# A four-layer graph network on one core: a fixed order for the hyperbolic preparation and end, and for the attention layer with its two GRUs

## The chip, the core and the metric

The kernel runs on one core of a Trainium2 chip. The metric is device time in microseconds (us) of one execution. Below, PE is the matrix engine (TensorE), DVE the vector engine (VectorE), ACT the scalar engine (ScalarE), POOL GpSimd, and SP the engine that issues most transfers.

## What is computed

N = 3327 nodes with D = 64 features and a 0/1 adjacency matrix of about 16 neighbours per row. Four layers follow each other, each of the form x = x + layer(relu(layernorm(x)), adj):

```python
# layers 0 and 3: hyperbolic, c = 1 and c = 1 / r**2
x_t = logmap0(h, c)
adj_att = sigmoid(x_t @ w[:D] + (x_t @ w[D:]).T + b) * adj
support = einsum('ij,ijd->id', adj_att, logmap(h[:, None], h[None], c))
out = proj(expmap(h, support, c), c)
# layer 1: decay
rank = cumsum(adj != 0, axis=1)              # weight 0.5 ** (deg - rank)
out = w @ (h @ weight) + bias
# layer 2: two GRU cells on sums over neighbours
edge_output = gru(concat(A_pos @ h, A_neg @ h), h, ...)   # adj has no negatives here
node_output = gru(softmax_mean(h @ W_gat), h, ...)
out = d_edge[:, None] * edge_output + d_node[:, None] * node_output
```

With a 0/1 matrix the attention is the mean of h @ W_gat over the neighbours without the diagonal, and the second half of the first GRU's input is zero.

## The kernel before

Nodes are padded to 3328 = 26 tiles of 128 (T = 26). X keeps the features as [128, 26, 64] in SBUF; the two halves of the tiles (HALVES, 13 each) are often handled one after the other. Shapes on DVE are thus 128x832 (half), 128x1664 (all), and 128x26 for one number per node.

`hyperbolic_series` (layers 0 and 3) has three parts. The preparation normalises (`norm_relu`, lines 111 to 129), computes |h|^2 (L386 to L388), scales to Xr (L399), splits it into two fp16 parts (L400, L405), transposes these to columns on PE (`to_columns16`, L407), computes the attention scalars left and right, spreads left over partitions into leftB (L452 to L463), and transposes a second set of columns, XE. Here the framework's scheduler orders the engines' instructions by its own costs. The series then runs over 4 column chunks times 26 row tiles with an order written out by hand (`manual_schedule`): sigmoid on ACT (L517), times adjacency on POOL (L519), two pairs of products on PE (L530, L531), a square on ACT (L537), two passes on DVE (L542, L543), and sums on PE (L552, L560). In layer 0 the adjacency tile comes by DMA (L505, 4 buffers), in layer 3 from fp8 masks that are already in SBUF. The end (L643 to L742) works on 128x26 numbers and then updates X by four wide passes per part (L739, L740); its square roots (`sqrt_`, L94) are corrected by one Newton step on DVE and are then inverted where 1/sqrt is wanted.

`plain_decay` (layer 1) loads 52 half-row tiles of the matrix (832 KB each, 4 buffers, L1259), makes fp8 masks on DVE (L1287), counts on DVE that entries are 0 or 1 (`zeros`, L1207; for 13 tiles, LATE, this is put off into layer 2, which loads them again, L1394), and runs cumulative counts, an exponential on ACT (L1300) and sums on PE (L1311). Its order is written out by hand. Before it, `norm_relu` and `split2` (L164) make the fp16 parts of h; POOL adds the bias to X in one instruction (L1362).

`plain_gat` (layer 2) normalises again, checks degrees (L1415, L1416), inverts them by DVE reciprocals (L1426), sums the masks times h on PE (L1407, 26 blocks of 16 products), and then runs two GRUs, each over 4 column blocks of 416 (L1437 to L1475): products (L1453, L1463), sigmoids (L1455), tanh (L1467), state (L1465 to L1475); for the second GRU first a product with W_gat (L1447) and a copy on ACT (L1448). All this is ordered by the scheduler. The GRU weights come by POOL's DMA queue at the start of layer 1 (`gru_weights`, L1209). `ball` (L274) prepares the constants of a hyperbolic layer, for layer 3 on DVE (L295 to L301). A last comparison of counts decides whether a slow fallback runs; it doesn't with these inputs.

## Time and profile before

| what | us |
|---|---|
| median of 3 runs (827.92 to 830.69) | 829.16 |
| the profiled execution's own time | 831.17 |
| its span (first to last instruction) | 829.5 |
| layer 0, preparation up to the first square's input | 0 to 33.5 |
| layer 0, series | 33.5 to 265.9 |
| layer 0, end | 265.9 to 284.3 |
| layer 1, first masks, normalising | 284.3 to 299.7 |
| layer 1, sweep up to its last product | 299.7 to 428.8 |
| layer 2, up to the first product of the mask sums | 428.8 to 457.8 |
| layer 2, mask sums | 457.8 to 497.0 |
| layer 2, GRUs; then the update of X | 497.0 to 538.7; to 543.0 |
| layer 3, preparation | 543.0 to 571.2 |
| layer 3, series | 571.2 to 801.9 |
| layer 3, end, and the close of the program | 801.9 to 822.1; to 829.5 |

A table row's borders are the starts of instructions in the timeline. Over the span PE is busy 662.2 us, DVE 721.5, ACT 562.0, POOL 419.0; these are averages over stages with different limits. In a timeline line the columns are start, busy time, engine, line of the kernel, operation, output and input with shapes, the count of merged instructions, and in brackets the idle time before and what ended it. The lines of a stretch table give the stretch, its length, then the busy time and number of instructions of PE, PE's weight loads, DVE, ACT and POOL, the granted PE clock, the DMA share and GB/s.

### The profile page before, as it was taken

The page shows a single profiled execution, that of the slowest core. Times are in us where ns is not written, and L with a number is a line of the kernel's source. Part 1 is how long each engine was busy: PE and PEld are TensorE (multiplying, and loading weights), DVE is VectorE, ACT ScalarE, POOL GpSimd, SP SyncE. Part 2 cuts the span into 40 slices and gives each one's busy share as a digit, 9 for nine tenths or more (in the row PEclk, how much of TensorE's full clock was granted, in tenths as well). Part 3 has the DMA queues.
Part 4 walks back from the last instruction along what each step waited for, and adds up shares of the span by engine and source line. Part 5 has one row for each costly group of instructions (what it writes and reads, how often), then busy time and mean ns, then how long its engine had stood idle before and what let it go on. Part 6 is the DMA issues. An engine that isn't in the chain of part 4 may idle for free.

```text
span 829.5 us, 11810 instructions
## 1 busy us (share of the span) xinstructions
PE 662.2 (80%) x4228; PEld 251.2 (30%) x4228; DVE 721.5 (87%) x1013; ACT 562.0 (68%) x684; POOL 419.0 (51%) x283
## 2 busy tenths in 40 slices
PE   0889999999896059989970997618999999998940
PEld 0422233333331024435430662204222333333310
DVE  7689999999997999999989946796999999999966
ACT  3878888888884167777761306448888888888850
POOL 2499989989985310002300000004787777787720
PEclk9999999999999569999995899958999999999985
DMA  2577766767662639999943630002001001000001
GB/s 42 167 235 227 204 204 191 238 182 204 190 191 66 225 126 339 349 347 333 338 170 126 220 113 1 0 0 48 1 2 35 1 1 35 0 2 1 0 4 44
DMA packets 56887, 107.86 MB, mean 130 GB/s; under 512 B 8305, under 2 KB 32817, under 8 KB 56817
## 3 DMA queue, kind: packets, MB, share of 16 engines
q1 hardware_dynamic: 51712, 106.68, 40.2%
q10 hardware_dynamic: 4656, 0.08, 0.3%
q8 instruction: 35, 0.57, 0.3%
q0 software_dynamic: 448, 0.24, 0.1%
q14 instruction: 36, 0.29, 0.1%
HBM read 103.73 MB, written 0.88 MB: 126 GB/s over the span
## 4 chain that ended last, share of the span: by engine, by line
DVE 65%; PE 14%; DMA 7%; ACT 6%; issue 5%; POOL 2%; ACTq 1%; DVEq 0%; POOLq 0%
DVE sig L543 22%; DVE slot L542 20%; DMA adj<-in 7%; DVE same L1207 5%; PE acc L1407 5%; DVE mask L1287 3%; POOL sig L519 2%; PE slot L552 2%; ACT y L537 1%; DVE deg L1426 1%; PE cnt L1294 1%; DVE X L740 1%; DVE prod L739 1%; PE slot L560 1%; DVE ln_v L123 1%
## 5 line engine op out<-in xcount | busy, mean ns | idle before, releaser
L537 ACT ACTIVATE y<-slot,shift_c 128x768 f32<-128x768 f32 (+1 forms) x208 | 197.6, 950 | 69.7 <-ACT sig L517 48.1
L543 DVE TENSOR_TENSOR sig<-slot,sig 128x768 f32<-128x768 f32 (+1 forms) x208 | 213.2, 1025 | 24.7 <-POOL sig L519 2.7
L542 DVE SCALAR_TENSOR_TENSOR slot<-y,slot 128x768 f32<-128x768 f32 (+1 forms) x208 | 212.1, 1020 | 9.0 <-ACT y L537 8.9
L519 POOL TENSOR_TENSOR sig<-adj,sig 128x768 f32<-128x768 f32 (+1 forms) x104 | 201.8, 1962 | 24.8 <-ACT sig L517 14.7
L517 ACT ACTIVATE sig<-leftB,right 128x768 f32<-128x768 f32 (+1 forms) x208 | 204.1, 981 | 0.2
L519 POOL TENSOR_TENSOR sig<-mask,sig 128x768 f32<-128x768 fp8e4 (+1 forms) x104 | 174.6, 1680 | 57.2 <-ACT sig L517 53.1
L552 PE MATMUL slot<-sig,Xr 128*64 128x384 f32 (+1 forms) x832 | 187.2, 538 | 18.3 <-DVE sig L543 18.3
L530 PE MATMUL slot<-XC,XT 128*128 128x384 f16 (+1 forms) x416 | 142.1, 342 | 5.0 <-DVE sig L543 3.3
L531 PE MATMUL slot<-XF,XE 73*128 73x384 f16 (+1 forms) x416 | 141.4, 340 | 0.0
L1300 ACT ACTIVATE w<-cnt,ebias 128x832 bf16<-128x832 f32 x104 | 93.8, 950 | 32.4 <-PE cnt L1294 32.4
L1207 DVE TENSOR_SCALAR_CACHE_REDUCE same<-adj 128x1664 bf16<-128x1664 f32 x52 | 97.7, 1880 | 3.5 <-DMA adj<-in 3.5
L560 PE MATMUL slot<-sig,X 128*32 128x384 f32 (+1 forms) x832 | 95.0, 529 | 0.0
L468 POOL COPY Xp<-Xe 128x234 f16<-128x234 f16 x2 | 0.8, 415 | 160.1 <-DVE XT L414 146.4
L552 PEld LDWEIGHTS slot<-sig,Xr 128*64 128x64 f32 x832 | 42.9, 135 | 123.9 <-DVE sig L543 85.2
L1294 PE MATMUL cnt<-mask,after 128*128 128x416 fp8e4 x208 | 54.8, 347 | 25.3 <-DVE mask L1287 22.6
L178 POOL TENSOR_TENSOR mask<-mask,offdiag 128x128 fp8e4<-128x128 fp8e4 x26 | 16.8, 666 | 105.4 <-PE cnt L1294 104.2
L530 PEld LDWEIGHTS <-XT 128*128 128x128 f16 x416 | 40.6, 98 | 94.7 <-issue 68.8
L1294 PE MATMUL cnt<-mask,rest 128*128 128x416 fp8e4 x208 | 55.0, 347 | 12.5 <-ACT w L1300 12.5
L1287 DVE TENSOR_SCALAR mask<-adj 128x1664 fp8e4<-128x1664 f32 x52 | 53.3, 1031 | 6.7 <-DMA adj<-in 6.6
L531 PEld LDWEIGHTS <-XE 73*128 73x128 f16 x416 | 40.7, 98 | 33.3 <-issue 9.3
L1311 PE MATMUL acc<-w,h 128*64 128x416 bf16 x416 | 47.2, 349 | 0.0
L1407 PE MATMUL acc<-mask,h 128*64 128x416 fp8e4 x416 | 38.3, 346 | 0.1
(293 smaller groups left out, 547.7 us busy)
## 6 DMA issues: line engine op xcount, KB each, us to landing
adj<-in SPq DMA_DIRECT2D x65, 832.0 KB, 6.9
adj<-in SPq DMA_DIRECT2D x78, 384.0 KB, 3.9
adj<-in SPq DMA_DIRECT2D x27, 512.0 KB, 4.7
leftB<-left SPq DMA_DIRECT2D x6, 384.0 KB, 3.9
XC<-XT SPq DMA_DIRECT2D x12, 96.0 KB, 3.0
X<-in SPq DMA_DIRECT2D x1, 832.0 KB, 4.5
out<-X SPq DMA_DIRECT2D x2, 416.0 KB, 2.4
XF<-XT SPq DMA_DIRECT2D x6, 96.0 KB, 2.7
```

What stands on the lines that cost most here:

```text
L517: A.activation(sig, leftB[c], AF.Sigmoid, bias=right[:, b:b + 1])
L519: G.tensor_tensor(sig, adj, sig, op=OP.mult)
L530: PE.matmul(L[:, o, :c[1] * P], XT[:, rows], XC[c][:, o, :], start=True, stop=False)
L531: PE.matmul(L[:, o, :c[1] * P], XE[:KE, rows], XF[c][:, o, :], start=False, stop=True)
L537: A.activation(ys[k], Ls[k][:, :, :c[1] * P], AF.Square, scale=-0.5 / SX ** 2, bias=shift_c)
L542: V.scalar_tensor_tensor(L, y, G3, L, op0=OP.add, op1=OP.mult)
L543: V.tensor_mul(sig, L, sig)
L552: PE.matmul(acc[c][o * D:(o + 1) * D, 0, :n], Xr[:, b, :], sigs[k][:, o, :], start=b == 0, stop=b == T - 1)
L560: PE.matmul(acc[c][q:q + 32, 1, :n], X0[:, b - 1 + i, :], w[:, o, :], start=b == 1, stop=b == T - 1, tile_position=(0, q))
L1207: V.tensor_scalar(same, adj, 0.0, 0.0, op0=OP.is_equal, op1=OP.add, accum_out=count)
L1294: PE.matmul(cnt[o][:, h, :BK], w, cols(k, o, h), start=w is after and steps[k][1] == T - 1, stop=True, skip_group_check=True)
L1300: A.activation(ws[k][:, o, :, :], cnt[o][:, :, :BK], AF.Exp, scale=-LN2, bias=ebias)
```

## The change

1. Hyperbolic preparation (both layers) goes into `manual_schedule` for ACT, DVE, PE and POOL. It no longer writes relu(H)/sd: R = max(H, 0) and its squares are summed, and 1/sd goes into the factor of Xr. `inverse_root` gives 1/sqrt directly with one Newton step. The fp16 copy into Xe goes from ACT to DVE. leftB is made from left itself instead of from its transposed copy, half of it copied by DVE. The small work for E, F and z is put between the DVE copies of the transposed columns. Numbers that the end needs are computed here. The first four adjacency tiles of layer 0 are loaded ahead of it; X comes in two transfers.
2. The end: fewer 128x26 steps, `inverse_root`, the Sqrt table loaded before in layer 3, X updated in halves, one product of the second half on ACT.
3. Weights of layers 1 and 2 come by SP's queue at the program's start, ahead of the first adjacency tiles; the constants of layer 3 are made on POOL in step 3 of the sweep.
4. Decay: 7 buffers instead of 4; bias added in 13 pieces on POOL in steps 3 to 15; second half normalised first, the lower fp16 part of the first half made in step 1; the degree total comes from ACT's accumulator.
5. Attention: fixed order for ACT, DVE and PE; 3 buffers for the late tiles; normalising first; W_gat is multiplied into the second GRU's weights ahead of the mask sums (the product L1447 goes); the degree check and 1/degree go to ACT (Relu with accumulator, Ln, Exp) with one Newton step on DVE; the half of the nodes that the mask sums need first is normalised first.
6. GRUs: the eight steps become a pipeline: products, sigmoids and the input of tanh of step u, with tanh and state of step u - 1.

```diff
+    def inverse_root(pool, src, name, root=None):
+        s0 = pool.tile(list(src.shape), F32, name=name) if root is None else root
+        if root is None:
+            A.activation(s0, src, AF.Sqrt)
+        q = pool.tile(list(src.shape), F32, name=name + "_q")
+        V.reciprocal(s0, s0)
+        V.scalar_tensor_tensor(q, src, -0.5, s0, op0=OP.mult, op1=OP.mult)
+        V.tensor_mul(q, q, s0)
+        V.scalar_tensor_tensor(s0, q, 1.5, s0, op0=OP.add, op1=OP.mult)
+        return s0
...
@@ hyperbolic_series, preparation
+            if masks is None:
+                for k in range(4):
+                    load(k)
-                norm_relu(tp, H)
...
+                    V.tensor_scalar(R[:, ts, :], H[:, ts, :], 0.0, None, op0=OP.max)
+                    A.activation(sr[:, ts, :], R[:, ts, :], AF.Square)
...
+                sd = inverse_root(tp, v, "sd", sd)
...
+                V.scalar_tensor_tensor(ia2, ia, 2.0, sd, op0=OP.mult, op1=OP.mult)
...
-                    V.tensor_mul(Xr[:, ts, :], H[:, ts, :], wide(ia2[:, ts]))
+                    V.tensor_mul(Xr[:, ts, :], R[:, ts, :], wide(ia2[:, ts]))
...
-                to_columns16(XT, Xp[:, :, :2 * D], P, 1)
+                to_columns16(XT, Xp[:, :, :2 * D], P, 1,
+                             (of_x0, of_e, of_f, lambda: V.tensor_copy(Xe[:, :, :D], hi), of_z))
...
+                to_columns16(XE, Xe, KE + 9, 0, (lambda: None, of_left))
...
@@ hyperbolic_series, end
+                last = HALVES[1]
+                extra = tp.tile([P, T // 2, D], F32, name="extra")
+                for k in range(T // 2):
+                    t = last.start + k
+                    A.activation(extra[:, k, :], M[:, t, :], AF.Copy, scale=am[:, t:t + 1])
...
@@ plain_decay
-                adjs[k] = wk.tile([P, 2, CW], F32, name="adj", bufs=4)
+                adjs[k] = wk.tile([P, 2, CW], F32, name="adj", bufs=AHEAD)      # AHEAD = 7
...
-                    if k == 4:
-                        G.tensor_tensor(X, X, bias[:, None, :].to_broadcast([P, T, D]), op=OP.add)
+                    if k == 1:
+                        late()
+                    if 3 <= k < 3 + T // 2:
+                        ts = slice(2 * (k - 3), 2 * (k - 2))
+                        G.tensor_tensor(X[:, ts, :], X[:, ts, :], bias[:, None, :].to_broadcast([P, 2, D]), op=OP.add)
...
@@ plain_gat
+                norm_relu(tp, hn, H.rearrange("p k o d -> p o k d"), order=(1, 0),
+                          then=lambda o: split2(*[p[:, :, o, :] for p in parts], H[:, :, o, :]))
+                PE.transpose(pt[:D, :D], wg, ident[:D, :D])
+                A.activation(wgT, pt[:D, :D], AF.Copy)
+                PE.matmul(pt[:D, :3 * D], wgT, wx[:D, :, :].rearrange("k g m -> k (g m)"), start=True, stop=True)
...
+                def inverse():
...
+                    V.tensor_scalar(deg, deg, 1.0, None, op0=OP.max)
+                    A.activation(few, deg, AF.Relu, bias=hundred, accum_out=ok[:, 3:])
+                    A.activation(r0, deg, AF.Ln)
+                    A.activation(r0, r0, AF.Exp, scale=-1.0)
+                    table_of(AF.Sigmoid, r0[:, :1])
+                    V.scalar_tensor_tensor(deg, deg, -1.0, r0, op0=OP.mult, op1=OP.mult)
+                    V.scalar_tensor_tensor(deg, deg, 2.0, r0, op0=OP.add, op1=OP.mult)
+                todo = {T - 4: lambda: turn(0), T - 6: lambda: degrees(0), T - 8: lambda: turn(4),
+                        T - 9: lambda: degrees(1), T - 11: lambda: turn(8), T - 12: lambda: degrees(2),
+                        T - 14: lambda: turn(12), T - 15: lambda: degrees(3), T - 17: inverse}
...
+                take(0)
+                for u in range(K + 2):
+                    if u < K:
+                        products(u)
+                    if u == 0:
+                        take(1)
+                    if u < K:
+                        sigmoids(u)
+                    if u == 0:
+                        take(2)
+                        take(3)
+                    if 0 <= u - 1 < K:
+                        tanh(u - 1)
+                    if u < K:
+                        before_tanh(u)
+                    if u < C:
+                        take2(u)
+                    if 0 <= u - 1 < K:
+                        state(u - 1)
...
-        nc.sync.dma_start(X, x.rearrange("p (t d) -> p t d", d=D))
+        for ts in HALVES:
+            nc.sync.dma_start(X[:, ts, :], x.rearrange("p (t d) -> p t d", d=D)[:, ts, :])
```

The new functions of the attention layer: `turn(t0)` is four transposes of H on PE and five copies on ACT; `degrees(k)` two products on PE and one subtraction on DVE; `take(k)` two ACT copies of the mask sums and one DVE product with 1/degree; `take2(k)` two ACT copies of that product; `products(u)` 8 products on PE into four of the eight PSUM banks in turn; `state(u)` three (first GRU) or four DVE passes.

## The prediction

> **What bounds the kernel now.** I read the chain of work that ended last, then busy time by stage, then the timeline of each stage that the change touches. The page's chain:
>
> ```profile
> DVE 65%; PE 14%; DMA 7%; ACT 6%; issue 5%; POOL 2%; ACTq 1%; DVEq 0%; POOLq 0%
> DVE sig L543 22%; DVE slot L542 20%; DMA adj<-in 7%; DVE same L1207 5%; PE acc L1407 5%; DVE mask L1287 3%; POOL sig L519 2%; PE slot L552 2%; ACT y L537 1%; DVE deg L1426 1%; PE cnt L1294 1%; DVE X L740 1%; DVE prod L739 1%; PE slot L560 1%; DVE ln_v L123 1%
> ```
>
> Over 40% is the two series, which the change leaves alone. The gains must lie between them; busy time by stage:
>
> ```profile
> 34.70:265.90 231.20, 215.63 (x1265) 67.93 (x1262) 211.01 (x224) 189.70 (x222) 207.03 (x112) 1.00 0.68 198
> 265.90:284.30 18.40, 0.00 (x0) 0.00 (x0) 16.95 (x72) 1.73 (x3) 10.15 (x17) 0.53 0.58 202
> 299.70:428.90 129.20, 125.58 (x840) 56.92 (x839) 119.71 (x131) 96.50 (x109) 16.81 (x26) 0.98 0.87 304
> 428.90:457.70 28.80, 5.15 (x29) 3.51 (x29) 27.78 (x35) 6.47 (x11) 0.00 (x0) 0.65 0.41 148
> 497.00:543.00 46.00, 31.19 (x163) 10.29 (x160) 31.54 (x57) 24.19 (x42) 0.00 (x0) 0.93 0.00 0
> ```
>
> From 428.9 to 457.7 PE does 5 us of work while DVE is full: the mask sums wait for DVE. From 497 no engine is full: the GRUs wait step by step. Timeline of DVE before the mask sums, its wait in the GRUs, the hidden stall in layer 1, and the table switches of the last end:
>
> ```profile
> 429.30 1.89 DVE L1415 TENSOR_SCALAR_CACHE_REDUCE few<-deg 128x1664 bf16<-128x1664 f32 x1 [2.56 <-ACT deg L1316]
> 431.12 1.88 DVE L1416 TENSOR_REDUCE zo<-deg 128x1 f32<-128x1664 f32 x1
> 443.49 2.74 DVE L1426 RECIPROCAL deg<-deg 128x416 f32<-128x416 f32 x1
> 524.32 0.65 DVE L1465 SCALAR_TENSOR_TENSOR nn<-ph,gb,spr 128x416 f32<-128x416 f32 x1 [0.68 <-PE ph L1463]
> 526.36 0.59 DVE L1469 TENSOR_TENSOR o<-hP,nn 128x416 f32<-128x416 f32 x1 [0.77 <-ACT nn L1467]
> 290.45 3.69 POOL L1362 TENSOR_TENSOR X<-X,bias 128x1664 f32<-128x1664 f32 x1 [8.01 <-DVE H L120]
> 292.38 1.79 DVE L124 TENSOR_SCALAR ln_v<-ln_v 128x26 f32<-128x26 f32 x1
> 804.76 1.28 ACT L98 ACT_TABLE_LOAD   x1 [2.89 <-DVE t L684]
> 806.29 1.28 ACT L687 ACT_TABLE_LOAD   x1
> ```
>
> A 128x26 step takes 0.18 us, yet L124 took 1.79: it ended as the bias addition did.
>
> **The Trainium skill.** "GPSIMD Engine Reference", section 1, says POOL shares its SBUF interfaces with DVE, contended by DVE's 2-port modes: L124 agrees, 1.61 us lost. "VectorE: DVE Perf Modes", section "The perf-mode tier table", gives fp32 tensor_scalar twice the rate of tensor_tensor: L1287 1.03 us against L1207's 1.88 for 1664 elements agrees, so R = max(H, 0) costs 0.5 us per half where L128 cost 0.98. "ScalarE: Activation LUTs", section "What ACT_TABLE_LOAD costs", gives 1283 ns plus a drain; the trace has 1.28 us and no drain (the next activation at 806.29 + 1.30), so I use 1.28. Its section "Table sets: the hidden batching unit" has ln and exp in one set; no run here shows it yet, so one load, two at the other end.
>
> **The change part by part**, against the profiled 831.17 us (span 829.5, 1.7 around it). On DVE a step that needs the one before starts 0.22 us after it, an independent one 0.10, a half (128x832) takes 0.98 (starts in the timeline).
>
> *Layer 0, preparation.* Now 5.36 (X landed) to 33.46 (first square). X in halves: 0.9 earlier (one 832 KB transfer lands in 4.5 us, a 416 KB one in 2.4, the second queued). Up to the second fp16 part: two passes L128 (1.95) become R (1.0), 0.95 saved; of the root and two reciprocals 0.8 goes beside sums: together 1.8. Then it is given back: in fixed order DVE does the dependent chain of E, F, z (of_x0 7 x 0.22, of_e and of_f 0.45 each, Xe 0.55, of_z 1.4, about 4.4 us) between copies of XT, where the scheduler now spaces 19 such steps at 0.1; and six of the seven XE groups, ahead of it now, come behind the leftB products on PE, 1.4. Before, ACT's Xe copy (1.58) and table load held its XT copies, which goes. Balance after the 1.8: +2.1. So +0.3 without, and -0.6 with X's 0.9. Then the first tiles: DVE idles 0.56 + 1.06 + 0.96 before three L543 between 43 and 51 us, POOL having waited for adjacency that was issued at 29.3; loaded ahead, about 1.5 goes, the rest is POOL's diag work. The 16 weight transfers ahead of these loads cost SP some 0.6 us each, 10 us; loads from 12 us on are hidden up to 33. **-2.1.**
>
> *Layer 0, end.* 265.93 to tanh 3.9 becomes 2.6 (kb, bx, bk precomputed; 9 dependent steps instead of 15); rr removes reciprocal and one product after tanh, 0.55; the last root 2.5 becomes 1.7 (inverse_root: one reciprocal, not two); the wide passes 7.4 become 7 x 0.98 = 6.9, ACT making the eighth (13 short activations at 0.25 = 3.3, hidden by 5.9 of DVE; uncovered it would cost the 1.0 that it saves). 1.3 + 0.55 + 0.8 + 0.5, rounded: **-3.3.**
>
> *Layer 1.* The bias leaves the path: -1.6; the lower part of the first half moves into step 1 of the sweep (-1.0, +1.0 there). In the sweep DVE does 48 more masks than the two made earlier, 50 x 0.94, and 39 checks x 1.80, 117.3, and additions 1.0; it waited 6.6 for adjacency (8 times) and 0.6 for PE. With 7 buffers and 33 us before the sweep, 9 tiles are in instead of 6; at 345 GB/s a tile takes 2.47 us against DVE's 2.37: the queue shrinks 0.1 x 43 = 4.3 us, less than it holds. So the 6.6 goes; next late is PE, 52 x 2.335 = 121.4 from about 296.5, and the pace of masks. 13 bias pieces (3.69 / 13 = 0.28 each) can hold a mask each: 0 to 3.7, I take 1. 1.6 + 6.6 - 1.0 rounds to **-7.3**.
>
> *Up to the mask sums.* With the sweep's last product at 428.8 as zero of time, X is final at 432.8 instead of about 434.1, L1415 and L1416 (3.77) gone from before it; the late tile's check (1.9, and 0.6 of waiting) goes behind; normalising undisturbed takes 8.0 to L128's start (542.96 to 550.98 in layer 3), so 440.8 instead of 453.85, the four reciprocals (10.9), L1424 and L1425 being out of it. PE's start doesn't gain all of it: its product with wgT waits for an ACT copy that stands behind the copy of the second half (H1 1.0, hi 0.95, lo 1.0, H0 1.0, hi 0.95: 445.9), then 0.7: 446.6 instead of 457.76. **-11.2.**
>
> *Mask sums.* 39.2, less 1.2 of waiting, plus 8 degree products 0.7: **-0.5**, end 485.3.
>
> *GRUs.* DVE's own steps: 4 takes 2.1, input of tanh 8 x 1.2, states 4 x 1.8 + 4 x 2.4: 28.5 us, where 41.7 passed. But DVE comes late: degrees(3) is on PE behind block 15 (472.3); then a check 1.8, maximum 1.0, and DVE waits for ACT's Relu, load, Ln, Exp (1.6 + 1.3 + 1.6 + 1.5 = 6.0; two loads 7.3), then 2 x 1.8, then the five last checks 9.3: 495.4, some 10 us after PE ended. Behind it stand the takes; step 1's products wait for take(3), as they use the banks of the sums. Takes to 497.5, tanh inputs of steps 0 and 1 and first state to 502.9, then 6 x 1.2 + 3 x 1.8 + 4 x 2.4 = 22.2, and 1.4 of bubbles and tail: 526.5, 41.2 after PE's end. **-0.5**; without the lateness it would be -6.
>
> *Layer 3.* Preparation as layer 0 without the halves, constants now ready: saves 1.8, gives 2.3 back: **+0.5** (bounds -2.5 if DVE's chain hides, +3). End: one table load and step savings up to tanh 1.9, last root 0.85, wide passes 0.95: **-3.7.** POOL's constants and memset cover: DVE work that doesn't need them.
>
> Sum -2.1 - 3.3 - 7.3 - 11.2 - 0.5 - 0.5 + 0.5 - 3.7 = -28.1. The profiled execution would take 803.1; the median stands 2.0 lower: 801.
>
> **The rivals.**
> *Fixed order costs* (809): each preparation gives back 3 more, and PE, not DMA, ends the sweep (2.3 x 52 plus a slow first step), so only 5 of 7.3 come: -28.1 + 6 + 2 = -20. For: only waits of 0.1 to 0.7 us are left to the scheduler there. Against: PE busy 125.6 includes slow-clock products before 304.
> *DVE in time* (793): Ln and Exp overlap the checks, so the GRUs gain 6, and the preparations 1.5 each: -37. Against: DVE's queue is in order.
> *Not what it says* (817): the pipeline and early mask sums are held by bank reuse; half of the 11.2 and 5 of the sweep lost: -12 to -18, -14 taken.
> *Slower* (835): PE's clock. In each series PE is busy 215.6 of 231.2 us at a granted 1.00; with fewer pauses before, the clock could fall. At 0.866 PE would need 249 per series, 17.8 more than now, twice 35.6, against 28.1 gained: about +7. It decides from 215.6/x = 245, a clock of 0.88. The page shows 0.9 or above all through both series but in slices at their borders: improbable.
>
> **The numbers.** Forecast 801: 0.47; fixed order 0.24; DVE in time 0.18; not what it says 0.07; slower 0.04. The range takes in the second and third with the unknown costs, 791 to 812. A measurement can tell some 0.3% (2.5 us) from no change. Faster 0.95, same 0.01, slower 0.04.
>
> **What would show it.** Right: L1426 and L1447 gone; first mask-sum product 17 to 19 us after the sweep's last (28.98 now); no DMA wait of L1287 over 0.5 us; DVE's last late check ending after the last mask-sum product, then GRU passes back to back; no L98 table load between 801.9 and tanh; the eight wide passes seven on DVE. Wrong: a preparation over 31 us from X to the first square; DVE waiting inside the GRU states; PE's clock under 0.9 in a series; a slow end that the chain gives to ACT.

## The result and the profile after

| kernel | median us | range, runs | ratio to before, 95% interval |
|---|---|---|---|
| before, same chip | 828.54 | 827.54 to 830.69, 4 | |
| changed | 819.63 | 818.34 to 820.25, 4 | 0.9882 [0.9868, 0.9897] |

Faster by 8.9 us in the medians. The forecast was 801: right in sign, but less than a third of the gain came. The profiled execution took 818.34 us (span 816.6), 12.8 less than the profiled one of before, which lay 2.6 above its median (831.17). First the chain of the changed kernel, then its stretches, with the columns as before.

```profile
DVE 31%; PE 7%; ACT 4%; issue 3%; DMA 1%; DVEq 0%; SPq 0%; ACTq 0%
```

```profile
36.21:268.38 232.17, 218.35 (x1268) 68.59 (x1265) 211.07 (x224) 190.82 (x224) 208.32 (x112) 0.99 0.66 190
268.38:283.85 15.47, 0.00 (x0) 0.00 (x0) 14.01 (x61) 4.94 (x16) 0.00 (x0) 0.53 0.91 346
296.79:425.33 128.54, 124.74 (x840) 56.89 (x839) 121.52 (x133) 97.48 (x113) 19.54 (x33) 0.99 0.79 286
425.33:443.63 18.30, 2.90 (x17) 2.03 (x18) 12.54 (x21) 7.09 (x12) 0.00 (x0) 0.71 0.37 140
484.58:531.13 46.55, 25.41 (x147) 8.84 (x144) 40.48 (x69) 22.99 (x41) 0.79 (x1) 0.79 0.11 37
```

The chain can be followed back over less than half of the span this time, so the stages carry the reading. The stretch ahead of the mask sums shrank from 28.80 to 18.30 as forecast. The sweep didn't: 128.54 against 129.20. In the last stretch DVE is now busy 40.48 of 46.55, where it had 31.54 of 46.00. Then the timeline, in the places shown of before:

```profile
291.89 0.18 DVE L138 TENSOR_SCALAR ln_v<-ln_v 128x26 f32<-128x26 f32 x1
293.72 1.25 DVE L143 SCALAR_TENSOR_TENSOR H<-H,ln_sd 128x832 f32<-128x832 f32 x1
295.65 5.69 POOL L1415 TENSOR_TENSOR X<-X,bias 128x128 f32<-128x128 f32 x8
480.80 1.89 DVE L1507 SCALAR_TENSOR_TENSOR deg<-deg,ln_sq 128x1664 f32<-128x1664 f32 x1 [7.70 <-ACT ln_sq L1505]
495.61 1.89 DVE L1248 TENSOR_SCALAR_CACHE_REDUCE same<-adj 128x1664 bf16<-128x1664 f32 x1 [2.35 <-DMA adj<-in]
497.43 1.58 DVE L1539 SCALAR_TENSOR_TENSOR deg<-bank,deg 128x416 f32<-128x416 f32 x3
796.97 1.28 ACT L119 ACT_TABLE_LOAD   x1
798.50 0.19 DVE L742 TENSOR_TENSOR th<-th,ti 128x26 f32<-128x26 f32 x1 [1.46 <-ACT spare L119]
```

The 1.79 of `ln_v` is 0.18: that stall is gone. The two passes L1415, L1416 and the reciprocals L1426 of before are gone, but DVE now waits 7.70 for ACT's inverse and 1.10 and 2.35 for two transfers, and reaches the takes at 497.43, 13 us after the mask sums. In the last end a wait of 1.46 is new. The ledger, from the timelines of the two profiled executions:

| stage | before | after | change | forecast |
|---|---|---|---|---|
| layer 0, to the first square | 33.46 | 36.21 | +2.75 | -0.6 |
| layer 0, series | 232.47 | 232.17 | -0.3 | -1.5 |
| layer 0, end | 18.41 | 15.47 | -2.9 | -3.3 |
| layer 1, first mask to last product | 144.44 | 141.48 | -3.0 | -7.3 |
| up to the first mask sum | 28.98 | 18.30 | -10.7 | -11.2 |
| mask sums | 39.24 | 40.95 | +1.7 | -0.5 |
| GRUs to the update of X | 41.84 | 42.42 | +0.6 | -0.5 |
| layer 3, preparation | 28.28 | 30.30 | +2.0 | +0.5 |
| layer 3, series | 230.94 | 231.72 | +0.8 | 0 |
| layer 3, end | 19.96 | 17.65 | -2.3 | -3.7 |
| update of X; close of the program | 4.12; 7.36 | 4.13; 5.80 | -1.6 | 0 |

That is -12.9 of span against -28.1. The mask sums end here where ACT takes the first of them, 0.5 before PE's last product ends, and layer 3's end begins at 802.18 in the kernel before. The close of the program is 1.6 shorter: this was not forecast, and why is not known. It took 7.4 and 7.6 us in the two profiles of the kernel before and of its variant below, and 5.5 to 6.0 in all others.

### The profile page after: what moved, and what is told of

Its sections match the earlier page's. It is cut to its first block, busy times and chain, and to the rows that moved or that the text cites. A ratio compares the mean times of both kernels' runs of the same rounds, so it can differ in the third digit from the quotient of the medians.

```text
span 816.6 us, 11802 instructions
## 1 busy us (share of the span) xinstructions
PE 659.8 (81%) x4215; PEld 252.1 (31%) x4215; DVE 709.1 (87%) x985; ACT 576.2 (71%) x729; POOL 416.1 (51%) x296
## 5 line engine op out<-in xcount | busy, mean ns | idle before, releaser
L577 POOL TENSOR_TENSOR sig<-adj,sig 128x768 f32<-128x768 f32 (+1 forms) x104 | 201.9, 1962 | 28.1 <-ACT sig L575 26.0
L191 POOL TENSOR_TENSOR mask<-mask,offdiag 128x128 fp8e4<-128x128 fp8e4 x26 | 15.0, 594 | 97.9 <-PE cnt L1333 97.9
L1518 PE MATMUL bank<-mask,h 128*64 128x416 fp8e4 x416 | 39.7, 348 | 0.0
```

The lines of the kernel that those rows point to most:

```text
L577: G.tensor_tensor(sig, adj, sig, op=OP.mult)
```

## The experiments

Every kernel is the changed one with the edit shown, unless said otherwise. Stage lengths are from each kernel's own profile; times are medians, with the ratio to the kernel before on the same chip.

### Yardstick: the changed kernel again

> The changed kernel once more, unedited, beside the others on one chip: what its stages do from run to run. From the runs so far: the first square between 36.2 and 37.6 us (the copies and transposes of the preparation ran at a varying granted clock), layer 1 between 141 and 144.5, the whole 818 to 822.

Measured: 819.45 us, 0.9889 [0.9873, 0.9906]. First square at 37.45, layer 1 143.1, the stretch up to the mask sums 19.7 (18.3 in the first profile), GRUs and ends as in the first profile to 0.3 us. So the first square of this preparation lies between 36.2 and 37.6 in the profiles that have it unedited, and a sweep moves by up to 2 us. The records of PE's granted clock say why. The first profile has one stretch of 3.4 us at 0.50 on the way to the first square (from 26.8 us) and none in the sweep; this one has 6.8 us there (from 26.6) and further stretches of 3.4 us in the sweep (365) and behind it (429). Small differences in these stages mean something only between profiles whose clock records are alike.

### The transfers of the sweep

Theory: TensorE sets the pace of the sweep, and DVE's waits for transfers were covered. Rival, the forecast's: the 6.6 us lay on the path.

```diff
-        AHEAD = 7
+        AHEAD = 4
```

> The changed kernel with layer 1's sweep loading 4 quarters of the adjacency ahead, as the kernel before did, in place of 7. Theory (PE sets the sweep's pace, 52 steps of 2.335 us, and DVE, which the transfers held up, had slack): VectorE waits for transfers again, 3 to 7 us in all, and the sweep's last product still comes 141 to 143 us after the first mask began (141.5 in the changed kernel); the whole time within 1 us of the changed kernel's. Rival (the prediction's: the 6.6 us of waits lay on the path): the sweep 4 to 7 us longer, 146 to 148, and the whole time with it.

Measured: 821.53 us, 0.9912 [0.9895, 0.9929]; layer 1 144.3 (clock 0.97). Waits for transfers came back, 3.2 us:

```profile
DVE mask L1326 <- DMA adj<-in: 3.2, 6, 1.0
```

The time lies 2.1 above the changed kernel run again, and the intervals allow 0 to 4. The sweep's length is neither the theory's 141 to 143 nor the rival's 146 to 148. The yardstick's sweep has the same single stretch of 3.4 us at half clock, and against its 143.1 this one is 1.2 longer: of 3.2 us of waiting, PE felt 1.2. The same question, asked the other way round on the kernel before (4 becomes 7 buffers and loads ahead, nothing else), is sharper:

> The kernel before with 7 quarters of the adjacency loaded ahead in layer 1 in place of 4, and nothing else of the change: this part alone. Theory (TensorE sets the sweep's pace, VectorE's waits for transfers were covered): VectorE's 6.6 us of waits for transfers go or nearly go, and the sweep's last product still comes 143 to 145.5 us after the first mask (144.4 before), the whole within 1.5 us of the kernel before. Rival (the prediction's): the sweep and the whole 4 to 6.6 us shorter.

Measured: 829.09 us against 829.58, 0.9993 [0.9985, 1.0000], at most 1.2 us gained. In the profiles layer 1 took 142.96 instead of 144.44, both sweeps at a full clock from 305 us on: four steps of PE that had taken 2.64 to 2.79 us took 2.34 like the others. The list of DVE's waits in layer 1 of the kernel before, and then of this one (who waited, for what: us in total, number of waits, the longest):

```profile
DVE mask L1287 <- DMA adj<-in: 6.6, 8, 1.2
DVE few L1415 <- ACT deg L1316: 2.6, 1, 2.6
```

```profile
DVE X L1320 <- PE acc L1195: 4.7, 1, 4.7
DVE few L1415 <- ACT deg L1316: 4.6, 1, 4.6
```

All 6.6 us of waiting for transfers are gone, and DVE waits for PE (4.7) and for ACT behind PE (4.6) instead. The rival falls: the waits were real, but most of them not on the path. Of 6.6 us, 0.5 came back in the medians and 1.5 in the one profile.

Is TensorE then the bound, and how far is the next? Half of the weighted sums left out, with 7 and with 4 loaded ahead:

```diff
-                        for i in range(2):
-                            for o in range(2):
-                                PE.matmul(acc[h][o * D:(o + 1) * D, :], parts[i][:, b, :], w[:, o, h, :],
-                                          start=b == T - 1 and i == 0, stop=b == 0 and i == 1)
+                        for o in range(2):
+                            PE.matmul(acc[h][o * D:(o + 1) * D, :], parts[0][:, b, :], w[:, o, h, :],
+                                      start=b == T - 1, stop=b == 0)
```

> The changed kernel with the second half (the low parts) of the sweep's weighted sums left out: 4 of the 16 wide products of a step fall away, so PE's step is about 1.75 us in place of 2.335; layer 1's sums lose their low parts. Theory (PE sets the pace and DVE, at 1.03 us for a mask and 1.96 for a check, is 4 us behind being the bound): the last product comes 2 to 4 us earlier, at 137.5 to 139.5 us after the first mask began, because VectorE's own work ends at 137.3 in the changed kernel and sets the end. Rival (DVE sets the pace already, PE only follows): 141 to 142, no gain. A gain near 30 us (52 x 0.58) would say that DVE doesn't bind at all.

> As the run with half the sums, and with 4 quarters loaded ahead in place of 7. With PE out of the way, VectorE is the bound, and its waits for transfers should now show in the length. Theory: 3 to 7 us of waits, and the last product 3 to 6 us later than in the run with half the sums and 7 loaded ahead. Rival (transfers never mattered here, they only fill slack of DVE's own making): within 1 us of it.

Measured: 816.56 us, layer 1 138.4; with 4 ahead 818.53, layer 1 139.5 with 2.4 us of waits. A quarter of PE's wide products away (some 30 us of its time by the expectation's sum) brought 3.1, and 4.7 against the yardstick: DVE stands right behind as the next bound. The fewer buffers then cost 1.1 us, between the two expectations, since the waits themselves were only 2.4. So even a shorter PE stage would have had little from the transfers.

### Four small waits

```diff
-        for ts in HALVES:
-            nc.sync.dma_start(X[:, ts, :], x.rearrange("p (t d) -> p t d", d=D)[:, ts, :])
+        nc.sync.dma_start(X, x.rearrange("p (t d) -> p t d", d=D))
...
-    params3 = ball(att3, b3, r3, math.sqrt(1e-15), 1e-15, of_r)
     hyperbolic_series(None, params, ok[:, 0:1])
+    params3 = ball(att3, b3, r3, math.sqrt(1e-15), 1e-15, of_r)
...
-                table_of(AF.Sqrt)
+                if r is None:
+                    table_of(AF.Sqrt)
...
                     A.activation(sq[:, ts, :], H[:, ts, :], AF.Square)
+                if r is not None:
+                    table_of(AF.Sqrt, sq[:, 0, :1])
...
-                    V.tensor_mul(th, th, ti)
+                    th0, th = th, new("th2")
+                    V.tensor_mul(th, th0, ti)
```

> The changed kernel with four edits in four stages that don't meet: X loaded in one transfer; layer 3's parameters loaded after layer 0 in place of before it (their four issues leave ACT's queue ahead of its first table load); the Sqrt table load of layer 3's preparation tied to its first squares, so that it can't run amid the attention; and the scaled tanh of layer 3's end written to a tile of its own. Theory: X lands at about 5.4 us in place of 6.4, and the wait of 1.4 us for the first squares goes, so the first square of the series comes 1.5 to 2.5 us earlier than 36.2; the second Sigmoid load goes and the GRUs' first gate comes up to 1.3 us earlier, or not at all earlier where VectorE's lateness sets it (it ends its checks at 497.4); the wait of 1.46 us at the end of layer 3 goes and that end is 1.2 to 1.5 shorter (17.65 to about 16.3). In all 3 to 5 us less than the changed kernel. Rival (these waits lie beside others): under 1.5 us in all.

Measured: 817.32 us, 0.9859 [0.9837, 0.9881], 2.1 below the changed kernel run again: less than the 3 to 5 expected, more than the rival's 1.5. The first square came at 35.5, 0.7 before the earliest of the changed kernel, where 1.5 to 2.5 was expected. X landed at 5.47, and the mean was ready at 7.45 as with two transfers (7.47): the halves neither win nor lose, because the second lands at 6.41, 1 us after the single transfer would. The first squares' sum began at 10.74 instead of 12.04, since ACT's table load no longer stood behind four DMA issues (6.91, not 9.73). The end of layer 3 took 16.30 instead of 17.65: the wait of 1.46 was a write after read, DVE overwriting `th` in place while a table load on ACT still had to read it. The stray Sqrt load in the attention went. There the changed kernel has five loads:

```profile
474.98 1.28 ACT L1504 ACT_TABLE_LOAD   x1
477.88 1.28 ACT L1505 ACT_TABLE_LOAD   x1
480.78 1.28 ACT L119 ACT_TABLE_LOAD   x1
482.30 1.28 ACT L119 ACT_TABLE_LOAD   x1
486.73 1.28 ACT L1565 ACT_TABLE_LOAD   x1
```

The fourth belongs to layer 3's preparation: with no input to wait for, the scheduler put it here, between the preload of Sigmoid and the gates, and Sigmoid was loaded again. Without it the GRUs didn't start earlier, as the expectation's second branch had it: DVE's lateness set their start.

### The place of the inverse

```diff
-                todo = {T - 4: lambda: turn(0), T - 6: lambda: degrees(0), T - 8: lambda: turn(4),
-                        T - 9: lambda: degrees(1), T - 11: lambda: turn(8), T - 12: lambda: degrees(2),
-                        T - 14: lambda: turn(12), T - 15: lambda: degrees(3), T - 17: inverse}
+                todo = {T - 1: lambda: degrees(0), T - 2: lambda: degrees(1), T - 3: lambda: degrees(2),
+                        T - 4: lambda: degrees(3), T - 5: lambda: r0.append(inverse()), T - 7: lambda: turn(0),
+                        T - 9: lambda: turn(4), T - 11: lambda: turn(8), T - 13: lambda: turn(12),
+                        T - 14: inverse_end}
```

`inverse_end` holds the two last passes of `inverse`.

> The changed kernel with the attention's fixed order altered and nothing else: the four degree steps right behind the first four pairs of tiles, the inverse's maximum and ScalarE chain behind the fifth, its two last VectorE passes behind the fourteenth, so that VectorE no longer stands 7.7 us behind Ln and Exp. Theory (the prediction's lateness of VectorE is real, and the inverse's place makes it): VectorE has 31.5 us of work and some 3.5 of waits for transfers in a stage whose mask sums take TensorE 41.4, so its checks end before them; the first take comes 42 to 44 us after the first mask sum in place of 53.8, the GRUs stay at 30 to 33, and the whole time falls by 8 to 11. Rival (the checks are paced by their transfers, three buffers of 832 KB): the take at 50 to 54, under 3 us gained.

Measured: 816.65 us, 0.9859 [0.9836, 0.9881], 2.8 below the changed kernel, where 8 to 11 was expected. DVE's checks ended 41.2 us after the first mask sum (53.9 before), but the mask sums themselves now took 47.0 to the end of the last product, not 41.4, and the take came at 47.6, between the two expectations. The timeline of PE shows why:

```profile
468.75 1.12 PE L1481 MATMUL bank<-ident,H 128*128 128x128 f32 x4 [4.38 <-ACT xh L1486]
```

A turn needs a bank that ACT empties, and ACT was in its chain of Relu, Ln and Exp. The wait had moved from DVE to PE. Second try, the turns behind that chain:

```diff
-                        ... T - 7: lambda: turn(0),
-                        T - 9: lambda: turn(4), T - 11: lambda: turn(8), T - 13: lambda: turn(12),
-                        T - 14: inverse_end}
+                        ... T - 11: lambda: turn(0),
+                        T - 14: lambda: turn(4), T - 17: lambda: turn(8), T - 20: lambda: turn(12),
+                        T - 13: inverse_end}
```

> The run with the early inverse again, with the four turns of H behind the eleventh, fourteenth, seventeenth and twentieth pair of tiles, that is after ScalarE's chain of Relu, Ln and Exp has ended, and the last two passes behind the thirteenth. Theory (in the first try VectorE was in time, but TensorE stood 5.6 us because the turns' banks waited for ScalarE): the mask sums take 41 to 42 us again and not 47.0, the first take comes 42 to 43.5 us after the first mask sum (53.8 in the changed kernel, 47.6 in the first try), the GRUs 31 to 33.5, the whole 810 to 813. Rival (the turns wait elsewhere, or the checks again end after the mask sums): the take at 46 or later.

Measured: 810.71 us, 0.9767 [0.9751, 0.9783]; mask sums 41.1 to the end of the last product, take at 41.8, all as expected; GRUs 33.0 (42.4). So the lateness of DVE was worth 8.7 us between the medians and 9.3 to 9.7 in the two stages of the profiles, and its cause was where `degrees`, `inverse` and `turn` stood in the fixed order, not DVE's work.

### The fixed order of the preparations

```diff
-            with tc.tile_pool(name="hsp", bufs=1) as tp, tc.tile_pool(name="hsps", bufs=2, space=PSUM) as ps, \
-                    tc.manual_schedule(engines={mybir.EngineType.Activation, mybir.EngineType.DVE,
-                                                mybir.EngineType.PE, mybir.EngineType.Pool}):
+            with tc.tile_pool(name="hsp", bufs=1) as tp, tc.tile_pool(name="hsps", bufs=2, space=PSUM) as ps:
```

> The changed kernel with both hyperbolic preparations ordered by the scheduler, as in the kernel before, with the changed kernel's passes: the fixed order alone is undone. Theory (the fixed order costs 1 to 2 us in each preparation, by the wait of 2.0 for the third VectorE copy behind seven small steps and the inverse root, and by the small numbers ahead of the first sigmoid): first square at 34 to 36 us in layer 0, layer 3's preparation 28 to 29.5 in place of 30.3. Rival (the order is good and the passes are what costs, or the scheduler does worse with them): 37 or more, and 30.3 or more.

Measured: 812.29 us, 0.9809 [0.9789, 0.9830], 7.2 below the changed kernel. First square at 34.3 (36.2 to 37.6), layer 3's preparation 25.96 (30.34), below the 28 that the theory allowed: the order costs more than it said. The changed kernel, layer 0 (DVE, then PE, then ACT):

```profile
26.45 0.19 DVE L475 TENSOR_TENSOR z<-rr,ax 128x26 f32<-128x26 f32 x1
26.67 0.24 DVE L476 TENSOR_SCALAR z<-z,isqc 128x26 f32<-128x26 f32 x1
26.82 0.42 DVE L486 COPY XT<-pt 128x512 f16<-128x512 f16 x1
27.29 0.32 PE L506 MATMUL pw<-wlr,XT 128*128 128x6 bf16 x6 [2.00 <-DVE XT L486]
28.32 2.02 PE L519 MATMUL junk<-ident,left 128*128 128x128 f32 x8
30.13 1.10 PE L519 MATMUL pe<-ident,left 128*128 128x128 f32 x8
35.15 1.15 ACT L575 ACTIVATE sig<-leftB,right 128x1024 f32<-128x1024 f32 x1 [1.73 <-DVE bh L544]
```

and the one with the scheduler's order:

```profile
25.37 0.17 DVE L536 TENSOR_TENSOR root<-root,rr 128x26 f32<-128x26 f32 x1
25.47 0.41 DVE L484 COPY XT<-pt 128x512 f16<-128x512 f16 x1
25.80 0.22 DVE L474 TENSOR_SCALAR z<-z,isqc 128x26 f32<-128x26 f32 x1
25.94 0.41 DVE L484 COPY XT<-pt 128x512 f16<-128x512 f16 x1
27.30 1.52 PE L482 MATMUL pt<-ident_h,Xe 128*82 128x128 f16 x21
28.65 1.11 PE L517 MATMUL junk<-ident,left 128*128 128x128 f32 x8
```

In the fixed order the third copy stands behind the whole chain of z, each step 0.22 after the last, and PE idles 2.0 us for it; the scheduler puts steps of independent chains between each other, 0.1 apart, and lets the copies through. It also does 25 of the 26 XE transposes ahead of the broadcasts, of which the fixed order has 18 after them; and in the fixed order the first sigmoid waits 1.73 for the last of the small numbers, which it doesn't read (presumably it takes memory that the preparation gives back).

The first eight broadcasts took 2.02 in the one and 1.11 in the other, and the granted clock accounts for it. In the changed kernel it was 0.50 from 26.8 to 30.2 us, and the next eight, at 1.00, took 1.10; with the scheduler's order it was 1.00 from 26.2 us on. In layer 0 and in layer 3, every profile with the changed kernel's preparation has a stretch of 3.4 or 6.8 us at 0.50 that falls on the first eight (1.66 to 2.08 us), and no profile with the scheduler's order has one there (1.11). So part of what the fixed order costs comes by way of the clock. That PE's idling brings these stretches was not tried.

Two other fixed orders, to see whether it is a fixed order as such. The first moves z behind the copies, the copy to Xe to ACT, and the small numbers (`X0` to `bh`) ahead of XE; beside it the bias became one POOL instruction again.

```diff
-                             (of_x0, of_e, of_f, lambda: V.tensor_copy(Xe[:, :, :D], hi), of_z))
+                             (of_x0, none, of_e, of_f))
+                A.activation(Xe[:, :, :D], hi, AF.Copy)
+                of_z()
...
-                    if 3 <= k < 3 + T // 2:
-                        ts = slice(2 * (k - 3), 2 * (k - 2))
-                        G.tensor_tensor(X[:, ts, :], X[:, ts, :], bias[:, None, :].to_broadcast([P, 2, D]), op=OP.add)
+                    if k == 3:
+                        G.tensor_tensor(X, X, bias[:, None, :].to_broadcast([P, T, D]), op=OP.add)
```

> The changed kernel with another fixed order in the preparations: the copy of the f16 tile goes to ScalarE and the inverse root behind the last copy of the transposes, so that VectorE copies come first; the small numbers stand before the transposes of the extra rows in place of behind everything. Beside it the bias of layer 1 is added by one GpSimd instruction in place of 13. Theory: left is ready about 1 us earlier, and the first sigmoid 1.5 us earlier for the small numbers' sake; first square at 34 to 35.5 in layer 0, layer 3's preparation 27.5 to 29. For the bias: GpSimd's 13 pieces of 0.69 us (9.0 in all) become one of 3 to 8 us; layer 1, which TensorE sets, stays within 1 us of 141.5 to 143 at a full clock. Rival: the order isn't what binds, and neither stage moves by over 0.5 us.

Measured: 816.16 us, 0.9854 [0.9824, 0.9885]. Layer 3's preparation 28.66, as expected; first square 36.33, outside the 34 to 35.5 expected. The bias in one piece held `ln_v` for 1.79 again, and the first weighted product of layer 1 came 17.2 us after the first mask, against 15.8 in every other profile of the changed kernel: 1.4 of the 1.6 forecast. At the sweep's end the clock hides this (144.05 here, 144.18 in the next run, without the bias in one piece but with 6.8 us at half clock instead of 3.4). The second order keeps this one (bias in 13 pieces again) and puts five groups of XE ahead of the broadcasts, the small numbers behind them:

```diff
-                to_columns16(XE, Xe, KE + 9, 0, (lambda: None, of_left))
+                to_columns16(XE, Xe, KE + 9, 0, (none,) * 4 + (of_left,))
```

> The changed kernel with a fixed order again, but another: as in the first other order (the f16 copy on ScalarE, the inverse root behind XT's copies), and the first five groups of transposes of the extra rows ahead of the sixteen broadcasts, where the changed kernel has two; the small numbers stand behind the broadcasts, while VectorE waits for them. Theory (this order costs, not a fixed order as such): layer 3's preparation 26 to 27.5 us against 30.3 in the changed kernel, 28.7 in the first other order and 25.6 in the scheduler's; first square 33.5 to 35. Rival (only the scheduler's interleaving of small steps helps): layer 3's preparation 28.5 or more.

Measured: 815.10 us, 0.9812 [0.9793, 0.9831]. Layer 3's preparation 27.04, inside the theory's range; first square 36.41, outside it. So it is this order rather than a fixed one that costs most in layer 3 (3.3 of 4.4 us come back), the clock included: it stays at 1.00 here from 551.8 us on, before the broadcasts, and falls to 0.50 on the second eight of them in the other two. In layer 0 PE holds both of these orders back: it works from 26.97 us to the series' first product at 35.28 without a pause, and slowly. The clock's record begins only at 32.8 and 33.0 us in these two runs, at 21.9 to 26.2 in the others; before that eight broadcasts took 2.02, and XE's transposes 0.118 us each, against 0.072 in the scheduler's order at 1.00. (A window table shows 1.00 for a stretch without a record.)

### What holds in layer 0: tables and SP's queue

```diff
-                table_of(AF.Sigmoid)
+                table_of(AF.Sigmoid, hi[:, T - 1, :1])
```

with the scheduler's order, and layer 3's Sqrt tied as in the four small edits.

> The run with both preparations ordered by the scheduler, with the table loads tied to what they are to follow: Sigmoid's to the f16 copy, and layer 3's Sqrt to its first squares. In the free order, Sqrt's and Sigmoid's loads ran back to back at the start of layer 0, and each was loaded again on the way (at 15.95 and 31.95 us). Theory: the squares' sum comes 1.3 to 1.6 us earlier and the reload ahead of the first sigmoid goes; first square at 31.5 to 33 us against 34.3, layer 3's preparation 25 to 26.2, the whole 1 to 3 us below 812.3. Rival (the loads lie beside other work): first square at 34 or later.

Measured: 811.49 us, 0.9769 [0.9751, 0.9787]. The reloads went and the first sigmoid ran at 28.65 instead of 33.24, but the first square came at 35.2: the expectation missed, and what the rival said (34 or later) came. PE's and SP's lines say what was late next:

```profile
17.48 10.19 SPq L369 DMA_DIRECT2D adj<-in  x5
27.78 2.64 SPq L385 DMA_DIRECT2D XC<-XT  x4
```

```profile
33.23 0.59 PE L589 MATMUL slot<-XC,XT 128*128 128x512 f16 x1 [3.45 <-DMA XC<-XT]
```

XT was ready at 24.0, but its way into XC went out at 27.78, behind sixteen weight transfers and the five adjacency tiles that these pushed to 17.5. In the kernel before nothing stood there (XC out at 26.40, the tiles after it). The weights moved behind layer 0 in the program:

```diff
-    wt, bias, wg, gru = middle_weights()
     hyperbolic_series(None, params, ok[:, 0:1])
+    wt, bias, wg, gru = middle_weights()
```

> The changed kernel with the weights of the middle layers loaded after layer 0's series in place of before its preparation, so that SP's queue has no sixteen transfers ahead of the adjacency tiles and the columns XC. Theory (the fixed order on the engines makes XT late, at 27.3, so the queue was not the limit yet): XC goes out right behind XT and the first square moves by under 0.7 us, 36 to 37.5. Rival (the queue is the limit): XC out 2 us or more earlier and the first square at 35 or earlier.

> The run with preparations ordered by the scheduler and tied table loads, and with the weights loaded late. There XT was ready at 24.0 us, XC went out at 27.78 behind the weights and the adjacency tiles, and TensorE waited 3.45 for it. Theory (SP's queue is the limit once the order isn't): XC out at 24 to 25, the wait under 1 us, the first square at 31 to 32.5 in place of 35.2, and the whole 2.5 to 4 us below 811.5. Rival (the transfers themselves are slow, not their place in the queue): first square at 34 or later.

Measured: with the fixed order 819.94 us, first square 37.08, no gain, as the theory had it; with the scheduler's order and tied tables 808.19, 0.9738 [0.9719, 0.9758], first square 31.29, inside the range, 3.9 earlier. Of these, 3.1 are PE's earlier first product (30.16 for 33.23); the other 0.8 are the clock, 0.50 behind the wait of 3.45 and 1.00 here. XC went out at 25.80, not at 24 to 25: SP isn't part of the fixed order, and the scheduler still put the weights ahead of XC, but the adjacency tiles first:

```profile
7.01 3.19 SPq L369 DMA_DIRECT2D adj<-in  x4
25.09 0.60 SPq L1270 DMA_DIRECT2D gb<-in  x1
25.80 3.12 SPq L385 DMA_DIRECT2D XC<-XT  x4
```

The tiles were long in by then, and PE no longer waited for XC. So the queue is a second bound in layer 0 that lay under the first.

### All together

The scheduler's order with tied tables, X in one transfer, layer 3's parameters late, the tanh in its own tile, the early inverse with late turns; then the same with the weights late.

> The changed kernel with all that gained: both preparations ordered by the scheduler with tied table loads, X in one transfer, layer 3's parameters loaded after layer 0, the scaled tanh in a tile of its own, and the early inverse with the later turns. If the parts add: first square at 30.5 to 32 us, the take at 42 to 43.5 after the first mask sum, layer 3's preparation 25 to 26.2, its end 16.3; 797 to 801 in all against 819.5 for the changed kernel. Rival (they share cover, or the earlier stages shift a transfer or a clock against the next): 803 or more.

> The run with all that gained, and the weights loaded late. XC went out at 26.4 there and TensorE waited 3.0 for it. Theory: first square at 29.5 to 31.5 in place of 33.2, the whole 794.5 to 796.5 in place of 798.1. Rival (the late weights delay layer 1's first tiles or its weights by as much): 797.5 or more.

Measured: 798.12 us, 0.9621 [0.9608, 0.9635], and 796.14, 0.9599 [0.9581, 0.9617]. First square at 33.2 and 30.9, take at 42.5 and 41.9, GRUs 31.9 and 31.8, layer 3's preparation 25.6 and 25.7, its end 16.3. The parts add. The first square of the first kernel missed its range by the wait for XC, 3.0.

## Why the prediction was right or wrong

Right: the sign, and three mechanisms with their sizes: up to the mask sums (-10.7 for -11.2; -9.3 in the yardstick, by its clock), layer 0's end (-2.9 for -3.3), and DVE late for the GRUs, 13 us where "some 10 us" was said. From 801 to 819.6, 15.2 us are stages that came out above the forecast, and the 1.6 of the close, which was luck, is already taken off. The other 3.4 are the way from profile to median: the forecast took 2.1 off, but the profiled execution of the changed kernel lay 1.3 below its median.

- **"So the 6.6 goes; next late is PE, 52 x 2.335 = 121.4 from about 296.5"** is the largest step that failed: layer 1 gained 3.0, not 7.3. PE was late already. By that sum it would have ended at 417.9. In the changed kernel its last product ended at 425.3: the first weighted product began at 299.7, and the 51 steps to the last group took 124.8, 2.34 each and 5.6 on top. Of these 5.6, 3.2 fall at the change from one half of the columns to the other, where PE waits for ACT's degree steps (two waits, 2.9 us together; 1.6 before). Right behind that change, at 357 to 365 us, a stretch of 3.4 us at half clock (once 6.8) shows in 12 of the 16 profiles of the changed kernel and its variants, and in neither of the two profiles of the kernel before. It made the yardstick's sweep 1.6 longer than the first profile's, so with it the gain is 1.3 and not 3.0. What brings it was not tried. The 6.6 us of waiting were worth 0.5 to 1.5. "PE, not DMA, ends the sweep" had been put among the rivals. What layer 1 gained at equal clocks is an earlier first weighted product (15.8 us after the first mask, 18.1 before), of which 1.4 are the bias, and 0.6 in PE's slow steps. POOL's 13 pieces took 0.69 us each, not 0.28, and DVE's H passes beside them 1.25 instead of 1.02, in line with the page "GPSIMD Engine Reference", section 1, of the Trainium skill, on the interfaces that POOL shares with DVE.
- **"Balance after the 1.8: +2.1"** was mis-sized. The passes saved what was said: from X to the start of the second fp16 part layer 3 went from 15.6 to 13.7. The order gave back more: from there to the first square 16.6, against 12.7 before. The chain of steps was priced, but not PE's idling for the copy behind it, the broadcasts at half clock and the sigmoid's wait for the last small number. It is 4.4 us in layer 3. In layer 0 it is at least 1.9, with 3.1 of SP's queue hidden under it.
- **"X's 0.9"** failed: the second half landed 1 us later than the whole had. And ACT's first table load went behind the DMA issues of layer 3's parameters, 1.3 us, a queue that the prediction didn't look at. **"loads from 12 us on are hidden up to 33"** was true of the loads and missed what stood behind them.
- **"about 1.5 goes"** in layer 0's series: 0.3 went. DVE's early waits for POOL fell from 2.6 to 0.8 us, but it waited 1.1 for ACT instead.
- **Mask sums, "less 1.2 of waiting"** failed: they took 1.7 more, not 0.5 less. PE had no waiting to lose, it was busy for all of the 39.24 us before. The degree products came as priced (0.7). Not priced were the turns: 13 transposes, 2.0 us, now stand between the sums, where 6 stood before (1.5), the other 7 ahead of them. The mask products themselves took 38.4 for 37.9. The clock is not the cause: it was 0.83 in the first 9 us, and 0.79 before.
- **GRUs, -0.5**: +0.6, near as it stands, but partly by luck. DVE came 2.8 later than summed: two waits for transfers, 3.5 us, were not in the sum, and ACT's chain was waited for 7.7, where 6.0 was put. From the first take on the stage was 1.5 shorter than summed (29.6 for 31.1). The rival "DVE in time" put 6 us on the lateness; the run with the inverse and the turns moved showed 8.7. The skill's page "ScalarE: Activation LUTs", section "Table sets: the hidden batching unit", has Ln and Exp in one set; here each loaded its own, 1.28 us twice, and the measurement decides.
- **Layer 3's end, -3.7**: 1.35 lost to the write after read on `th`; without it the end is 3.7 shorter, as forecast.

Two slips in the prediction carry no weight: L1207, which it sets beside the page's tensor_tensor, is a tensor_scalar with a count (a tensor_tensor half takes 1.02 and gives the same ratio, and R took 0.55 per half), and sums of 3.15 and 7.2 became 3.3 and 7.3.

Of the rivals, "Fixed order costs" (809) had both of the causes that mattered most. Its 6 for the preparations came to 4.9 against the forecast, its 2 for the sweep to 4.3; the series, the mask sums, the GRUs and layer 3's end, which it left as forecast, made up most of the rest.

## What to carry to other kernels

A wait that the profile shows on an engine with slack is no gain until the engine behind it has been asked when it finishes: give the waiting engine what it waits for, alone, and look for the new waits. A fixed order must be written for the consumer that is late next: copies that another engine waits for go ahead of chains of small steps, chains are interleaved, and a long ACT chain has to be placed against everything that needs ACT, turns of banks included. Instructions without an input (table loads, weight transfers) go where the scheduler likes: tie them to what they are to follow, and read each queue, SP's and ACT's too, in front of what is urgent. Before two profiles of a stage are compared, compare their records of the granted clock: one stretch of 3.4 us at half clock made a sweep 1.6 longer, as much as several of these edits were meant to gain.

## What the runs showed of the hardware

- Ln and Exp on ACT each brought a table load of 1.28 us (474.98 and 477.88).
- Small DVE steps of 128x26 take 0.18 to 0.19 us; the next begins 0.22 us after one that it depends on, and 0.08 to 0.12 where another chain's step stands between.
- A transfer of X of 832 KB landed at 5.4 us, two halves of 416 KB at 4.3 and 6.4.
- Eight fp32 broadcasts (128x128) on PE took 1.11 us at a granted clock of 1.00 and 2.02 at 0.50 (prep_free and the changed kernel). In the changed kernel's preparations the record falls to 0.50 for 3.4 or 6.8 us at a time.
- On POOL an addition of 128x1664 took 3.69 us, and 13 of 128x128 took 0.69 each, 9.0 in all.
